# Summing a node's first twelve edges by tile additions in a graph network kernel

## The chip, the cores and the metric

The kernel runs on one core of a Trainium2 chip. The metric is the time of one execution on the device in microseconds, the median of several. PE is TensorE, DVE VectorE, ACT ScalarE, POOL GpSimd, and SP the engine that starts most plain transfers. PEld is PE's loading of weights. L480 means line 480 of the kernel that the profile belongs to, so the same line number means different things before and after.

Each set of runs was given a chip that could not be chosen, and the kernel before met two kinds of them: on one kind it takes about 9670 us, on the other about 8980 us. Within a kind the runs of one kernel agree to about one per cent. I call them the slow and the fast kind. The prediction and the first result are from the slow kind. Numbers are compared only within a kind, except where the text says that it compares the kinds.

## The reference

There are N = 10000 nodes with D = 512 features, and 160000 edges sorted by target, each with one of four types. Layer 0 sends messages of the right type over each edge; layer 1 is two steps of mean aggregation.

```python
h = relu(layernorm(x))
h_all = einsum('nd,rdf->nrf', h, rel_W) + rel_b         # four tables: (10000, 4, 512)
agg = segment_sum(h_all[src, edge_type], dst) / max(deg, 1)
x1 = layernorm(h + h @ self_W + self_b + agg)
x = x + layernorm(x1 + gelu(x1 @ W1 + b1) @ W2 + b2)
h = relu(layernorm(x))
for W_self, W_neigh, b in ((ws1, wn1, bs1), (ws2, wn2, bs2)):
    agg = segment_sum(h[src], dst) / max(deg, 1)
    h = relu(h @ W_self + agg @ W_neigh + b)
out = x + h
```

## The kernel before

The work falls into four stages: products (five 512 x 512 weights for 79 blocks of 128 nodes, into `hall_d`), a pass of sums over `hall_d` with the feed-forward, and a pass each over `h1_d` and `h2_d`. The edge lists are prepared on DVE between the first products and the others. In every pass the sum of a block's edges is the same function: up to 18 gathers of 128 rows, each split in a high and a low part for two fp32r matmuls by a one-hot matrix.

```python
def block_sums(b, table, idx):
    n = caps[b]                                   # 18
    hot = hotp.tile([P, CAP, P], F32R, name="hot")
    nc.vector.tensor_tensor(hot[:, :n], lane..., loc[:, at[b]:at[b] + n]..., op=OP.is_equal)
    pa = psA.tile([P, D], F32, name="pa")
    for t in range(n):
        rows = rowp.tile([P, D], F32, name="rows")          # 12 buffers
        nc.gpsimd.indirect_dma_start(out=rows, in_=table, ...idx[:, w:w + 1]...)
        nc.scalar.copy(hi, rows)
        nc.vector.tensor_tensor(lo, rows, hi.bitcast(F32), op=OP.subtract)
        nc.tensor.matmul(pa, hot[:, t, :], hi, start=(t == 0), stop=False)
        nc.tensor.matmul(pa, hot[:, t, :], lo, start=False, stop=(t == n - 1))
    return pa

# products, of one block (cut)
    for j, w in enumerate([wself] + wrel):
        pm = psM.tile([P, D], F32, name="pm")               # 4 buffers in PSUM
        for k in range(KC):
            nc.tensor.matmul(pm[:r], hT[:, k, :r], w[:, k, :], ...)
        nc.vector.tensor_tensor(ha[:r, j - 1, :], pm[:r], brel[...], op=OP.add)
# feed-forward: for a group of four blocks in one piece, after their four sums (cut)
```

The read-out of `pm` by DVE is what matters later: PE has four such buffers, and if DVE does not read them, PE stands.

## Time and profile before

| what | before |
|---|---|
| median of three runs, profiled span | 9659.56 us, 9616.8 us |
| products end | 2010 us |
| first gather of `hall_d` to first of `h1_d` | 3213 us |
| from there to the end | 4389 us |
| PE, DVE, ACT, POOL busy | 74%, 52%, 34%, 51% |

The table says which stage takes how long, and the shares say that no engine is full over the whole. The prediction shows the same stages engine by engine, and reads from them which engine limits which stage.

### The profile page before, as it was taken

The page shows a single profiled execution, that of the slowest core. Times are in us where ns is not written, and L with a number is a line of the kernel's source. Part 1 is how long each engine was busy: PE and PEld are TensorE (multiplying, and loading weights), DVE is VectorE, ACT ScalarE, POOL GpSimd, SP SyncE. Part 2 cuts the span into 40 slices and gives each one's busy share as a digit, 9 for nine tenths or more (in the row PEclk, how much of TensorE's full clock was granted, in tenths as well). Part 3 has the DMA queues.
Part 4 walks back from the last instruction along what each step waited for, and adds up shares of the span by engine and source line. Part 5 has one row for each costly group of instructions (what it writes and reads, how often), then busy time and mean ns, then how long its engine had stood idle before and what let it go on. Part 6 is the DMA issues. An engine that isn't in the chain of part 4 may idle for free. (4 is left out here: it accounts for less than half of the span.)

```text
span 9616.8 us, 69806 instructions
## 1 busy us (share of the span) xinstructions
PE 7076.1 (74%) x18796; PEld 3705.1 (39%) x18796; DVE 4980.6 (52%) x6861; ACT 3224.2 (34%) x5464; POOL 4946.0 (51%) x4465
## 2 busy tenths in 40 slices
PE   6208999977777777686777767767766777777677
PEld 2103444433333333343334444444443444444344
DVE  6994222244545454545454555555554555555555
ACT  0000000023334343333343444444443444444444
POOL 1001111144546464646463767767665767777666
PEclk8558999978787878787877878888888888888888
DMA  3002222254545454545353666666665666666666
GB/s 110 23 0 92 96 101 109 84 169 135 147 129 154 137 159 132 152 122 165 113 167 111 198 181 194 188 185 194 187 177 179 201 198 201 201 204 204 192 198 181
DMA packets 498906, 1459.78 MB, mean 152 GB/s; under 512 B 90419, under 2 KB 90419, under 8 KB 488371
## 3 DMA queue, kind: packets, MB, share of 16 engines
q0 software_dynamic: 337680, 1106.78, 39.4%
q1 hardware_dynamic: 109330, 191.42, 6.2%
q10 hardware_dynamic: 51488, 157.01, 4.1%
q8 instruction: 150, 2.46, 0.1%
q14 instruction: 258, 2.11, 0.1%
HBM read 1249.45 MB, written 205.45 MB: 151 GB/s over the span
## 5 line engine op out<-in xcount | busy, mean ns | idle before, releaser
L313 POOL DMA_INDIRECT rows<-h_d,idx x2814 | 3038.9, 1080 | 1383.8 <-issue 756.4
L319 DVE TENSOR_TENSOR lo<-rows,hi 128x512 fp32r<-128x512 f32 x4221 | 2803.5, 704 | 1798.0 <-issue 449.5
L318 ACT CAST hi<-rows 128x512 fp32r<-128x512 f32 x4221 | 2467.0, 618 | 3592.9 <-PE pa L320 1612.6
L321 PE MATMUL pa<-lo,hot 128*128 128x512 f32 x4221 | 2321.8, 551 | 537.1 <-DVE lo L319 335.6
L313 POOL DMA_INDIRECT rows<-hall_d,idx x1407 | 1600.7, 1138 | 1444.3 <-DVE lo L319 873.9
L320 PE MATMUL pa<-hi,hot 128*128 128x512 f32 x4221 | 2016.5, 478 | 439.1 <-issue 232.8
L321 PEld LDWEIGHTS pa<-lo,hot 128*128 128x128 f32 x4221 | 909.2, 215 | 1367.0 <-DVE lo L319 647.1
L320 PEld LDWEIGHTS pa<-hi,hot 128*128 128x128 f32 x4221 | 920.9, 218 | 945.1 <-issue 654.5
L187 PE MATMUL pm<-wrel,hT 128*128 128x512 f32 (+1 forms) x2528 | 1115.8, 599 | 42.2 <-DVE xs L193 25.7
L422 PE MATMUL po<-wns,mTb 128*128 128x512 f32 (+1 forms) x1264 | 788.3, 781 | 205.0 <-ACT mTb L150 126.9
L187 PEld LDWEIGHTS pm<-wrel,hT 128*128 128x128 f32 (+1 forms) x2528 | 481.7, 191 | 661.3 <-issue 605.1
L419 PE MATMUL po<-wss,hTb 128*128 128x512 f32 (+1 forms) x1264 | 690.1, 630 | 0.7 <-ACT hTb L150 0.7
L181 POOL TENSOR_TENSOR hg<-hg,bself 128x512 f32<-128x512 f32 (+1 forms) x79 | 99.5, 1280 | 1129.5 <-PE pT L149 1129.5
L149 PE MATMUL pT<-ident,mb 128*128 128x128 f32 (+1 forms) x632 | 142.7, 366 | 708.8 <-ACT mb L414 491.5
L190 DVE TENSOR_TENSOR ha<-pm,brel 128x512 f32<-128x512 f32 (+1 forms) x316 | 218.2, 691 | 764.6 <-PE pm L187 764.6
L306 DVE TENSOR_TENSOR hot<-lane,loc 128x2304 fp32r<-128x2304 f32 (+1 forms) x237 | 602.8, 2544 | 5.6 <-PE pa L320 5.4
L368 PE MATMUL ph<-x1T,w1s 128*128 128x512 f32 (+2 forms) x1344 | 570.6, 586 | 27.0 <-ACT x1T L150 19.1
L422 PEld LDWEIGHTS po<-wns,mTb 128*128 128x128 f32 (+1 forms) x1264 | 308.6, 256 | 636.5 <-issue 448.1
L375 PE MATMUL po<-w2s,hid 128*128 128x512 f32 (+1 forms) x1264 | 548.1, 594 | 0.0
L377 DVE TENSOR_TENSOR xsg<-po,xsg 128x512 f32<-128x512 f32 (+1 forms) x79 | 54.6, 691 | 903.9 <-PE po L375 903.9
L425 DVE TENSOR_TENSOR ob<-po,bss 128x512 f32<-128x512 f32 (+1 forms) x158 | 109.3, 692 | 728.4 <-PE po L422 653.3
L182 POOL TENSOR_TENSOR xg<-xg,ln2b 128x512 f32<-128x512 f32 (+1 forms) x79 | 98.9, 1282 | 648.0 <-ACT hg L178 648.0
(96 smaller groups left out, 4032.9 us busy)
## 6 DMA issues: line engine op xcount, KB each, us to landing
hall_d<-ha ACTq DMA_DIRECT2D x78, 1024.0 KB
rows<-h_d,idx POOLq DMA_INDIRECT x2814
hb<-h_d SPq DMA_DIRECT2D x156, 256.0 KB
rows<-hall_d,idx POOLq DMA_INDIRECT x1407
h_d<-ob ACTq DMA_DIRECT2D x78, 256.0 KB
res<-xn_d SPq DMA_DIRECT2D x78, 256.0 KB
out_dram<-ob ACTq DMA_DIRECT2D x78, 256.0 KB
xg<-in_x_dram SPq DMA_DIRECT2D x19, 1024.0 KB
```

What stands on the lines that cost most here:

```text
L187: nc.tensor.matmul(pm[:r], hT[:, k, :r], w[:, k, :], start=(k == 0), stop=(k == KC - 1))
L190: nc.vector.tensor_tensor(ha[:r, j - 1, :], pm[:r], brel[:r, (j - 1) * D:j * D], op=OP.add)
L306: nc.vector.tensor_tensor(hot[:, :n], lane[:, None, :].to_broadcast([P, n, P]), loc[:, at[b]:at[b] + n].unsqueeze(2).to_broadcast([P, n, P ...
L313: nc.gpsimd.indirect_dma_start(out=rows, out_offset=None, in_=table, in_offset=bass.IndirectOffsetOnAxis(ap=idx[:, w:w + 1], axis=0))
L318: nc.scalar.copy(hi, rows)
L319: nc.vector.tensor_tensor(lo, rows, hi.bitcast(F32), op=OP.subtract)
L320: nc.tensor.matmul(pa, hot[:, t, :], hi, start=(t == 0), stop=False)
L321: nc.tensor.matmul(pa, hot[:, t, :], lo, start=False, stop=(t == n - 1))
L368: nc.tensor.matmul(ph[:, :n], w1s[:, k, f * P:(f + 1) * P], x1T[:, k, :n], start=(k == 0), stop=(k == KC - 1))
L375: nc.tensor.matmul(po[:r], hid[:, f, c * r:(c + 1) * r], w2s[:, f, :], start=(f == 0), stop=(f == FC - 1))
L419: nc.tensor.matmul(po[:r], hT[:, k, :r], wss[:, k, :], start=(k == 0), stop=False)
L422: nc.tensor.matmul(po[:r], mT[:, k, :r], wns[:, k, :], start=False, stop=(k == KC - 1))
```

## The change

Its intent is to leave most of the one-hot work out. A node's first 12 edges are gathered so that edge j of node p lands on partition p of tile j; tiles are then summed with plain additions. Only the further edges of a block (room for 720, six tiles) go through the one-hot, with plain fp32 matmuls. To find each node's first edge, the ends of the runs of equal targets are found by twelve top-eight passes, scattered to memory, read back and spread by a running maximum. That work is issued step by step between the products. The feed-forward is cut into quarters that go between the sums.

```diff
+    T = 3 * E // (4 * N)                    # 12
+    OV = 720
+    def edges(ep, ep2, pse):                # a generator: one step after each block of products
 ...
+        for j in range(n8):                 # 96 scatters of run ends
+            st = nc.gpsimd.indirect_dma_start(out=end_d, ...to_i[:, j:j + 1]..., in_=end_f[:, j:j + 1])
+        yield
+        nc.sync.dma_start(eb, end_d[:NE, :]...)
+        nc.vector.tensor_tensor_scan(run, eb, eb, 0.0, op0=OP.max, op1=OP.max)
 ...
+        for b in range(NB):                 # 79 gathers of 12 records a node
+            nc.gpsimd.indirect_dma_start(out=row0[:, b, :], in_=rec_d, ...first_i[:, b:b + 1]...)
 ...
+                for t in range(len(ov_tiles(b))):      # 469 gathers of one record a partition
+                    nc.gpsimd.indirect_dma_start(out=ovr0[:, b, t:t + 1], in_=rec_d, ...)
+            if b0 == 0:
+                nc.vector.copy_predicated(row0, few, nowhere...)
+        yield
+        nc.vector.tensor_scalar(ovr1[:, :NB - 1, :], ovr0[:, :NB - 1, :], 2, None,
+                                op0=OP.logical_shift_right)
 ...
         def products(g):
 ...
-                nc.gpsimd.tensor_tensor(h, h, bself[:r], op=OP.add)
+                nc.vector.tensor_tensor(h, h, bself[:r], op=OP.add)
+                next(step, None)
 ...
+        def fold(b, halves, left):
+            nc.vector.tensor_tensor(t[:r], t[:r], u[:r], op=OP.add)           # 3072 columns
+            while n > left:
+                nc.vector.tensor_tensor(t[:r, :m, :], t[:r, :m, :], t[:r, n - m:n, :], op=OP.add)
 ...
+        for i, (o, n) in enumerate(others):
+            nc.tensor.matmul(pa[:r], hot[:n, i, :r], o[:n], start=(i == 0), stop=(i == last))
 ...
+            for bs in plan:                 # a quarter of the feed-forward after each block's sum
+                    if queue:
+                        fed = queue.pop(0)()
```

## The prediction

> **What bounds the kernel now.** I read the page's slices, then a table of busy time by stage, then the groups, then stretches of the timeline. The stages follow from the first and last instruction of a line: products with the five weights (line 187) end at 2010 us, gathers from hall_d run from 2014.8 to 5143, those from h1_d from 5227.9, those from h2_d from 7441 to 9591. Cut there (columns: stretch, its length, busy us of PE, PEld, DVE, ACT, POOL, granted clock, DMA share, GB/s):
> ```profile
> 0.00:274.00 274.00, 187.25 (x420) 81.23 (x421) 172.07 (x344) 19.39 (x31) 35.48 (x33) 0.89 0.33 116
> 274.00:766.00 492.00, 47.30 (x169) 40.02 (x167) 492.00 (x157) 0.59 (x1) 3.77 (x3) 0.51 0.00 0
> 766.00:2012.00 1246.00, 1235.12 (x3050) 554.82 (x3050) 291.94 (x516) 90.75 (x148) 159.92 (x129) 1.00 0.25 99
> 2012.00:5228.00 3216.00, 2410.19 (x5746) 1204.58 (x5747) 1642.90 (x2562) 1215.08 (x1997) 1707.91 (x1487) 0.79 0.47 143
> 5228.00:7441.00 2213.00, 1604.65 (x4703) 926.48 (x4701) 1184.97 (x1644) 946.58 (x1643) 1521.67 (x1407) 0.82 0.64 186
> 7441.00:9616.00 2175.00, 1591.53 (x4710) 897.93 (x4710) 1196.66 (x1642) 951.84 (x1644) 1517.20 (x1407) 0.84 0.67 199
> ```
> Four limits show. Row two: DVE is busy all 492 us, with the products waiting behind it. Row three: PE is full at clock 1.00. Row four: nobody is full. The last two: POOL is at 69 and 70%. But POOL is closer to its limit than that share says, because the issue gap between gathers isn't counted as busy. Two stretches of POOL's timeline (start, duration, instruction, idle before it and its cause):
> ```profile
> 5238.01 0.95 POOL L313 DMA_INDIRECT rows<-h_d,idx  x1 [0.30 <-issue]
> 5239.26 0.95 POOL L313 DMA_INDIRECT rows<-h_d,idx  x1 [0.30 <-DMA rows<-h_d,idx]
> ...
> 2160.72 0.95 POOL L313 DMA_INDIRECT rows<-hall_d,idx  x1 [0.30 <-issue]
> 2211.55 0.95 POOL L313 DMA_INDIRECT rows<-hall_d,idx  x1 [49.89 <-DVE lo L319]
> ```
> An undisturbed gather costs POOL 0.95 + 0.30 = 1.25 us whatever it moves. Eighteen make 22.5 us a block of 128 nodes, 1755 us for 78 blocks. In the second stretch POOL stands 49.89 us: the twelve row buffers are full while PE works through the feed-forward of four blocks in one piece. That is the first pass's excess over the other two.
>
> The groups give the rest (busy, mean ns, idle before):
> ```profile
> L313 POOL DMA_INDIRECT rows<-h_d,idx x2814 | 3038.9, 1080 | 1383.8 <-issue 756.4
> L319 DVE TENSOR_TENSOR lo<-rows,hi 128x512 fp32r<-128x512 f32 x4221 | 2803.5, 704 | 1798.0 <-issue 449.5
> L313 POOL DMA_INDIRECT rows<-hall_d,idx x1407 | 1600.7, 1138 | 1444.3 <-DVE lo L319 873.9
> L306 DVE TENSOR_TENSOR hot<-lane,loc 128x2304 fp32r<-128x2304 f32 (+1 forms) x237 | 602.8, 2544 | 5.6 <-PE pa L320 5.4
> ```
> The mean gather is 1080 or 1138 ns, not 946 (the median). The timeline shows why; of both engines, in one stretch:
> ```profile
> 2288.43 2.52 DVE L306 TENSOR_TENSOR hot<-lane,loc 128x2304 fp32r<-128x2304 f32 x1
> 2288.61 3.17 POOL L313 DMA_INDIRECT rows<-hall_d,idx  x1 [0.30 <-DVE mvb L138]
> ```
> A gather that started just after a DVE operation with two SBUF inputs ended some 0.8 us after that operation, 2.2 us late.
>
> **What the Trainium skill says.** "SBUF — State Buffer", section "Who interferes with whom": a DVE instruction with two SBUF inputs contends with a GpSimd instruction that reads SBUF, and the later one blocks. The trace agrees: the stretch of (1.080 - 0.946) x 2814 + (1.138 - 0.946) x 1407 = 647 us. "TensorE: Matmul & The Clock Gate", section "What's actually happening": idle throttles PE, activity releases it. Agrees: 0.51 beside an idle PE, 1.00 beside a full one. So the clock of 0.8 in the passes is a sign of PE's slack and not a fixed price. "FP8 and Floating Point Precision" says that true fp32 takes four passes through the array. In the trace a fp32 512-column matmul is two instructions (2528 records for 1264 matmuls), which start 0.43 us apart at full clock, so 0.86 us; a fp32r one starts 0.23 us after another, which agrees roughly (3.7 times).
>
> **The change, part by part.**
>
> Gathers: still 12 + 6 = 18 a block (the last block 13 instead of 3), the same 1.25 us each. That floor doesn't move, and it decides.
>
> Edges and products. Removed from DVE: 78 comparisons of 1250 columns (1.45 us) and 78 pairs of one-hot and reduction (2.55 + 4.0 us), 624 us in all. Added: 12 top-eight passes with replacement, an estimate of 12 x 3 = 36 us from 1250 columns at 1.45 us a sweep, and 79 comparisons of 768 columns, under 1 us each. Two adds a block (2 x 0.69) come from POOL. All of it is issued between blocks of products; DVE had only 292 us of work in 1246 us of products, so PE keeps its 17.9 us a block (40 x 0.43 plus transposes): 27 + 79 x 17.9 = 1441 us. PE also gets 474 narrow matmuls, some 50 us. POOL gets 96 scatters and 79 + 469 small gathers, 644 x 1.25 = 805 us, from about 200 us on: hidden, unless DVE waits for the scatters in order (up to 100 us). Products end at about 1510 us instead of 2010: 500 us saved.
>
> Passes over h1 and h2. DVE loses 18 x 0.70 us of remainders and 2.55 us of one-hot a block, ACT 18 x 0.62 us of casts; neither was the bound. PE: 36 fp32r at 0.23 = 8.4 us become (6 + 3) x 0.86 = 7.7 us: no change. DVE gets the fold: 3072 columns, then 1536, at the one-hot's rate (2304 columns in 2.55 us) 3.3 and 1.7 us, both with two SBUF inputs. A gather comes to its read every 1.25 us, on average 0.6 us after the first add began; so it is held 3.3 - 0.6 = 2.7 us, and the next by 0.3 us in the second add. The smaller one-hot costs 0.3 us. So 22.5 + 3.3 = 25.8 us a block, 78 x 25.8 + 13 x 1.25 = 2030 us, plus 28 us from the last gather to the next pass: 2058 instead of 2213 and 2055 instead of 2175. Saved: only 155 + 120 us.
>
> Pass over hall_d. PE needs per block 12 x 0.43 for the sums, 32 x 0.43 for a quarter of feed-forward and 1.1 for transposes: 20.0 us at full clock, 23.5 at 0.85. POOL needs 22.5 + 3.0 for the fold + 0.9 for the last small adds and the 0.7 us operations of the norms: 26.4 us, and loses b2's add (1.39 us). The quarter between two sums is shorter than the two blocks of gather buffers (45 us), so the 49.9 us stands should go. With 0.6 us for PE nearly level with POOL: 27 us x 78 + 16 = 2122 us, plus a drain of five quarters, about 85 us as against 85 today (5143 to 5228). So 2207 instead of 3216: 1010 us saved.
>
> Sum: 1510 + 5 + 2207 + 2058 + 2055 = 7835 us; I say 7830.
>
> **Rivals.**
> 1. No lock loss: the fold is one long operation a block instead of 18 short ones, and gathers slip between. Then 22.5 us a block and 3 x 1770, about 7000 us. Against it: the 2.52 us one-hot above held its gather to the end.
> 2. The lock holds across the whole chain of adds, not to the end of each: the fold costs 4.4 us in the last two passes and 6 in the first, 27.2 and 29.5 us a block: about 8250 us. For it: gathers of up to 11.25 us in the first pass, and 2293.45 held 7.58 us by adds back to back. Against it: counted over the trace, 206 of the 228 gathers over 1.5 us ended 0.82 us after the end of the first such operation that they met. I weigh it at one in five.
> 3. PE becomes the bound in the first pass: at clock 0.8 it needs 25 us and waits for the last gather of a block before the quarter starts. Pass one goes to 29 or 30 us a block, in all about 8050 us. For it: the old clock of 0.79. Against: the clock rises when PE has no long idle.
> 4. The transfers: 18 gathers move 4.6 MB in 26 us, with loads some 215 GB/s; the third pass already moves 199 at a DMA share of 0.67. Not the bound.
> 5. The edge work doesn't hide: DVE stands at the read-back of the run ends, products end at 1650, in all 7970 us.
>
> **Range and chances.** Rival 2, 3 and 5 lie above, 1 below; half of rival 1 and all of 2 in the range: 7350 to 8250 us. For a change within 2% nearly all the first pass's and the edges' 1500 us must come back, which nothing here suggests; only a failed fit (the data miss the 720 slots and the general branch runs) would. Faster 0.98.
>
> **What would show it.** Right: no stretch of DVE alone before the products, PE full until about 1500; POOL's idle before gathers near 0.30 us each in all passes, no wait near 50 us; the gathers' mean 1.10 to 1.15 us, with one of about 3.5 us a block beside the fold. Wrong: gathers' mean under 1.0 (rival 1) or over 1.25 us (rival 2); POOL waiting for the fold or PE in the first pass (rival 3); PE idle at 200 to 500 us (rival 5).

## The result, and the profile after

| | before | after | predicted for after |
|---|---|---|---|
| median | 9678.06 us | 8584.87 us | 7830 us |
| products end | 2010 us | 2210 us | 1510 us |
| pass over `hall_d` | 3213 us | 2181 us | 2207 us |
| the last two passes | 4389 us | 4157 us | 4113 us |

The changed kernel is right in its outputs and faster: ratio 0.8873, interval 0.8821 to 0.8925. A ratio is the mean time of one kernel's runs over that of the other's of the same rounds, so not quite the ratio of the medians quoted. But the time lies far above the range that I gave. The table tells where: the three passes came out within 2% of their predicted lengths, and the products came out 700 us too long, longer even than before. This is the table of busy time by stage of the changed kernel (columns as in the prediction), cut where POOL starts and stops issuing the small transfers of the edge work:
```profile
147.00:224.00 77.00, 0.27 (x2) 0.06 (x1) 3.31 (x5) 0.58 (x1) 58.40 (x62) 0.53 0.10 28
224.00:340.00 116.00, 112.25 (x269) 50.28 (x269) 34.04 (x71) 6.46 (x11) 5.56 (x6) 0.95 0.21 82
340.00:440.00 100.00, 41.15 (x119) 17.21 (x118) 13.30 (x27) 2.00 (x4) 75.37 (x79) 0.68 0.11 26
440.00:556.00 116.00, 110.17 (x459) 51.89 (x458) 56.96 (x105) 8.88 (x15) 0.00 (x0) 0.94 0.28 109
556.00:865.00 309.00, 66.94 (x180) 26.21 (x179) 14.55 (x23) 1.17 (x2) 233.84 (x240) 0.57 0.04 7
865.00:975.00 110.00, 92.73 (x351) 42.06 (x351) 44.31 (x80) 9.50 (x15) 0.43 (x1) 0.85 0.27 104
975.00:1269.00 294.00, 89.30 (x172) 37.33 (x170) 18.21 (x32) 4.40 (x7) 223.15 (x229) 0.64 0.07 20
1269.00:2214.00 945.00, 906.22 (x2236) 405.63 (x2236) 272.45 (x469) 67.50 (x110) 0.05 (x2) 0.98 0.24 95
2214.00:4395.00 2181.00, 1698.10 (x3862) 748.70 (x3862) 1242.84 (x1672) 458.10 (x652) 1627.44 (x1417) 0.90 0.66 206
4395.00:8552.00 4157.00, 2899.51 (x6616) 1243.39 (x6616) 1144.32 (x789) 289.55 (x474) 3232.71 (x2834) 0.84 0.66 200
```
The reader is to compare the first number after each length (PE) with the fifth (POOL). Where POOL issues, PE does 0.27 of 77, 41 of 100, 67 of 309 and 89 of 294 us. In the rows between, where POOL has nothing to do, PE is busy 84 to 97% of the time. The last two columns say that it is not the memory: the transfers move next to nothing there. The granted clock falls to 0.53 to 0.68 in the same rows, as it did beside an idle PE in the prediction's table (0.51). It is too little to be the cause: a step of 0.43 us would take 0.81 us at 0.53 of the clock (an estimate from these numbers), and the steps shown next are 2.80 us apart.

So the products, which were to hide the edge work, stood while it went on. The question is why. Two stretches of that time, DVE's and PE's (start, duration, instruction, and in brackets the idle time before it and what ended it):
```profile
167.25 0.69 DVE L420 TENSOR_TENSOR ha<-pm,brel 128x512 f32<-128x512 f32 x1 [19.71 <-remote]
189.65 0.69 DVE L420 TENSOR_TENSOR ha<-pm,brel 128x512 f32<-128x512 f32 x1 [21.71 <-remote]
```
```profile
645.89 1.01 PE L417 MATMUL pm<-wrel,hT 128*128 128x512 f32 x1 [1.79 <-issue]
648.69 1.01 PE L417 MATMUL pm<-wrel,hT 128*128 128x512 f32 x1 [1.79 <-issue]
```
DVE reads out a product every 22.40 us, which is eight matmuls (four fp32 ones, two instructions each) 2.80 us apart; at full speed they are 0.43 us apart. And in this stretch PE waits for nothing that the profile shows ("issue"). This looked like an engine that gets its instructions slowly, and it led me first to theory S: **TensorE steps slowly as long as GpSimd issues small transfers**. Its rival, theory W, is the fifth rival of the prediction: **an instruction in DVE's order waits for a small transfer, and the read-out of the products stands behind it.**

The passes first, since there the prediction's steps can be seen to hold. The gathers and the first addition on the page (busy us, mean ns of one, idle before):
```profile
L453 POOL DMA_INDIRECT half<-h_d,row x1896 | 1902.3, 1003 | 719.4 <-issue 568.6
L453 POOL DMA_INDIRECT half<-hall_d,row x948 | 1072.5, 1131 | 1250.2 <-DMA ovr<-rec_d,at_i 945.6
L461 POOL DMA_INDIRECT other<-h_d,ovr x938 | 1330.4, 1418 | 285.8 <-issue 280.9
...
L480 DVE TENSOR_TENSOR half<-half 128x3072 f32<-128x3072 f32 (+1 forms) x237 | 795.7, 3358 | 703.3 <-DMA half<-h_d,row 308.8
```
And one block's additions with the gathers beside them, in the timeline:
```profile
6006.99 0.94 POOL L461 DMA_INDIRECT other<-h_d,ovr  x1 [0.30 <-issue]
6007.79 3.36 DVE L480 TENSOR_TENSOR half<-half 128x3072 f32<-128x3072 f32 x1 [4.43 <-DMA half<-h_d,row]
6008.24 3.73 POOL L461 DMA_INDIRECT other<-h_d,ovr  x1 [0.30 <-issue]
6011.19 1.76 DVE L483 TENSOR_TENSOR half<-half 128x1536 f32<-128x1536 f32 x1
6012.28 1.49 POOL L461 DMA_INDIRECT other<-h_d,ovr  x1 [0.30 <-issue]
```
An undisturbed gather still costs 0.94 + 0.30 us, and one that starts 0.45 us into the first addition takes 3.73 us, to 0.82 us after the addition's end. The next one is held to the end of the second addition in the same way, each by its own operation. The time that the gathers of the last two passes take above 945 ns each sums to (1.003 - 0.945) x 1896 + (1.418 - 0.945) x 938 = 554 us, 3.5 us for each of 158 blocks; I had predicted 3.3.

### The profile page after: what moved, and what is told of

Its sections match the earlier page's. It is cut to its first block, busy times and chain, and to the rows that moved or that the text cites.

```text
span 8551.8 us, 44099 instructions
## 1 busy us (share of the span) xinstructions
PE 6091.4 (71%) x14444; PEld 2657.9 (31%) x14444; DVE 2916.0 (34%) x3393; ACT 858.3 (10%) x1306; POOL 5490.2 (64%) x4911
## 5 line engine op out<-in xcount | busy, mean ns | idle before, releaser
L493 PE MATMUL pa<-other,hot 128*128 128x512 f32 (+2 forms) x2814 | 1808.9, 793 | 1587.8 <-DMA other<-h_d,ovr 848.8
L453 POOL DMA_INDIRECT half<-h_d,row x1896 | 1902.3, 1003 | 719.4 <-issue 568.6
L453 POOL DMA_INDIRECT half<-hall_d,row x948 | 1072.5, 1131 | 1250.2 <-DMA ovr<-rec_d,at_i 945.6
L461 POOL DMA_INDIRECT other<-h_d,ovr x938 | 1330.4, 1418 | 285.8 <-issue 280.9
L493 PEld LDWEIGHTS pa<-other,hot 128*128 128x128 f32 (+2 forms) x2814 | 653.8, 251 | 2598.0 <-issue 1842.4
L480 DVE TENSOR_TENSOR half<-half 128x3072 f32<-128x3072 f32 (+1 forms) x237 | 795.7, 3358 | 703.3 <-DMA half<-h_d,row 308.8
L364 POOL DMA_INDIRECT ovr<-rec_d,at_i x469 | 457.5, 975 | 371.7 <-DVE at_i L361 225.7
L461 POOL DMA_INDIRECT other<-hall_d,ovr x469 | 554.9, 1183 | 143.2 <-issue 113.6
L483 DVE TENSOR_TENSOR half<-half 128x1536 f32<-128x1536 f32 (+2 forms) x395 | 525.9, 1331 | 13.6
L496 PE MATMUL pa<-half,ident 128*128 128x512 f32 (+1 forms) x948 | 438.1, 598 | 2.2 <-DVE half L483 2.2
```

What stands on the lines that cost most here:

```text
L364: nc.gpsimd.indirect_dma_start(out=ovr0[:, b, t:t + 1], out_offset=None, in_=rec_d, in_offset=bass.IndirectOffsetOnAxis(ap=at_i[:, b - b0, ...
L453: nc.gpsimd.indirect_dma_start(out=t[:r, j, :], out_offset=None, in_=table, in_offset=bass.IndirectOffsetOnAxis(ap=row[:r, b, i * H + j:i ...
L461: nc.gpsimd.indirect_dma_start(out=o[:n], out_offset=None, in_=table, in_offset=bass.IndirectOffsetOnAxis(ap=ovr[:n, b, t:t + 1], axis=0))
L480: nc.vector.tensor_tensor(t[:r], t[:r], u[:r], op=OP.add)
L483: nc.vector.tensor_tensor(t[:r, :m, :], t[:r, :m, :], t[:r, n - m:n, :], op=OP.add)
L493: nc.tensor.matmul(pa[:r], hot[:n, i, :r], o[:n], start=(i == 0), stop=(i == last))
```

## The experiments

Eighteen kernels were run, and all were correct.

### 1. Do gathers issued beside the products slow TensorE? (fast kind, kernel before 8968.76)

The kernel before with bself's and ln2b's additions on DVE as after (p0), and with 474 gathers added whose result nobody reads: of 4-byte rows (p1), of 2048 bytes (p2), of 512 bytes (p3).
```diff
-                nc.gpsimd.tensor_tensor(h, h, bself[:r], op=OP.add)
+                nc.vector.tensor_tensor(h, h, bself[:r], op=OP.add)
+        for j in range(474):                              # p1; p2, p3 with wider rows
+            nc.gpsimd.indirect_dma_start(out=junk[:, j:j + 1], in_=rec_d, ...idx1[:, j:j + 1]...)
```

> Control for the three probes: the kernel before, with the two adds a block of the products stage moved from POOL to DVE, so that POOL does nothing there. All theories: the stage from 766 us to the last product stays about 1246 us, at clock 1.00, and the whole stays near 9620 us; DVE has over 900 us of slack in the stage.

> The control plus 474 gathers of 4-byte rows, 128 rows each, into a column that nothing reads, issued by POOL back to back beside the products; nothing of PE, DVE or ACT waits for them. Theory A (indirect DMAs with tiny rows slow PE itself while POOL issues them): PE makes a quarter of its normal progress for the 590 us that they take, so the products end some 400 us later and the whole is near 10,000 us. Rival B (in the changed kernel PE was held by the order of the edge work on DVE and its waits, the gathers do nothing): no change, within 30 us of the control.

> The control plus 474 gathers of 2048-byte rows from x into tiles that nothing reads, in the same place. Theory A with the row size as the cause: no slowing, as in the passes, where PE runs 34 matmuls in a row beside such gathers: within 50 us of the control. If any indirect DMA beside full PE load slows PE: some 400 us more, as with 4-byte rows.

> The control plus 474 gathers of 512-byte rows. If there is a step between 4 and 2048 bytes, this says on which side 512 lies: either about 400 us later than the control or within 50 us of it. I expect it nearer to the 2048-byte case.

Measured: 8999.11, 8969.12, 9001.38 and 8975.91 us; the products end at 2003, 2002, 2011 and 2005 us. Nothing slowed by more than 8 us. Two flaws keep these runs from settling it. The gathers ran from 287 us on, and more than half of them beside a PE that was idle anyway. And, as showed only in the next set, this was the fast kind of chip.

### 2. The additions cut, and fewer gathers (slow kind, kernel before 9673.5, three rounds)

The changed kernel again (r0); the fold's additions cut into pieces of 512 columns (a1); room for 640 further edges of a block in place of 720, so 17 gathers a block in place of 18 (a3; the fullest block of these data has 637); both (a5).
```diff
-            nc.vector.tensor_tensor(t[:r], t[:r], u[:r], op=OP.add)                 # a1, a5
+            for i in range(n):
+                nc.vector.tensor_tensor(t[:r, i, :], t[:r, i, :], u[:r, i, :], op=OP.add)
-    OV = 720                                                                        # a3, a5
+    OV = 640
```

> The changed kernel itself again, beside the kernel before, which took 8969 us here and not 9678. Theory A' (the products stage stalls through something of the changed kernel's own, its tiny indirect DMAs beside its order of waits): the products end near 2210 us again, PE doing one instruction in 0.7 to 1.4 us while POOL scatters and gathers. Rival C (the stall belongs to the chip of the first measurement, as does part of its slower passes): the products end near 1500 us as I predicted, and the whole comes to 7800 us.

> The changed kernel with every add of the fold cut into adds of 512 columns: the same work on DVE (some 0.3 us more a block), in operations of 0.6 us instead of 3.3 and 1.7. Theory L (a gather is held to the end of the one DVE operation that it meets): the mean of the gathers from h falls from 1003 (halves) and 1418 ns (others) to under 1050 both, the block from 26.3 to about 24 us, the last two passes together from 4157 to about 3800 us. Rival M (the hold lasts over a chain of adds back to back): no gain, the one held gather a block still takes 4 to 5 us.

> The changed kernel with room for 640 instead of 720 further edges a block (the data's fullest block has 637): five gathers of further edges instead of six, 17 a block instead of 18. If POOL's 1.25 us a gather bounds the passes: 78 x 3 x (1.25 + a little hold) = about 300 us less in all, 100 us a pass. If PE bounded the first pass: nothing there, about 200 us in all. The products stage gets 78 gathers less, at most 90 us.

> Both edits. If both count on POOL they add: about 300 + 400 us less than the changed kernel in the passes. The first pass stops at PE's 20 us a block at full clock, near 23 us at the granted one, so it may gain less.

| | median us | ratio to before | products end | pass over `hall_d` | last two passes |
|---|---|---|---|---|---|
| r0_same | 8590.12 | 0.8881 | 2209 | 2215 | 4159 |
| a1_split | 8857.35 | 0.9161 | 2209 | 2481 | 4113 |
| a3_ov640 | 8187.96 | 0.8469 | 2099 | 2138 | 3930 |
| a5_both | 8311.28 | 0.8589 | 2098 | 2312 | 3905 |

The first result repeats: products to 2209 again. One gather fewer a block is worth 402 us here. In the profiled runs it is 110 in the products (78 small gathers fewer), 77 in the first pass and 229 in the other two. In these two POOL's 1.25 us an issue make 156 x 1.25 = 195 of it. Cutting the additions did what it should to the hold: the mean of a further gather of `h_d` fell from 1438 to 939 ns. And yet the kernel became 267 us slower. Its trace shows POOL and PE in one stretch of the last pass but one:
```profile
6007.75 0.95 POOL L453 DMA_INDIRECT half<-h_d,row  x1 [0.30 <-issue]
6014.67 0.94 POOL L453 DMA_INDIRECT half<-h_d,row  x1 [5.98 <-PE pT L160]
```
```profile
6010.00 0.27 PE L160 MATMUL pT<-ident,hb 128*128 128x128 f32 x1 [1.68 <-issue]
6012.10 0.37 PE L160 MATMUL pT<-ident,hb 128*128 128x128 f32 x1 [1.83 <-issue]
6013.50 0.37 PE L160 MATMUL pT<-ident,hb 128*128 128x128 f32 x1 [1.03 <-issue]
6014.20 0.37 PE L160 MATMUL pT<-ident,hb 128*128 128x128 f32 x1 [0.33 <-issue]
```
PE's four small transposes start 2.10, 1.40 and 0.70 us apart, multiples of 0.70, although nothing that the profile shows holds them; the next four, of mb, start 0.67 us after these and take 1.12 us together. POOL then waits for PE. So theory S's slow steps turn up in the passes as well. Summed over the three passes, the idle time of PE that `prof <label> --waits` puts down to issue grows from 584 us in r0 to 905 in a1 (from 498 in a3 to 754 in a5), while the time that the gathers of the last two passes take above 945 ns each falls from 562 to 81 us. That fits a loss by slow steps. Whether it is one, or the price of more and shorter additions, set 5 tells.

### 3. The changed kernel on the fast kind (kernel before 8985.03)

The changed kernel (r1); p1's gathers again, but made to depend on the degrees, so that all run from 799 to 1398 us beside products at full clock (p4); the changed kernel with an addition of 256 columns on POOL after each of the 644 small transfers (a6); the changed kernel with all the edge work issued before the products (a2).
```diff
+        nc.vector.tensor_scalar(idxj, idx1[:, :474], late, None, op0=OP.add)     # p4; late from rdeg
+            nc.gpsimd.tensor_tensor(pad, zero[:, :256], col..., op=OP.add)        # a6, 644 times
-        next(step)                                                                # a2: moved down
-        for g in groups:
-            products(g)
         for _ in step:
             pass
+        for g in groups:
+            products(g)
```

> The changed kernel once more, to see which kind of chip this call got: the first call's chip ran the kernel before in 8969 us, the second call's in 9674. Where the kernel before takes 9650: 8590 us and products that end at 2210. Where it takes 8970: if PE's slow steps are the chip's, products near 1500 us and a whole of 7800; if they are the kernel's, 2210 again.

> The first probe put right: its 474 gathers of 4-byte rows ran half beside an idle PE. Now their indices wait for the degrees, so that all run beside the products at full clock. Theory S (on such a chip PE falls to steps of 0.7 us while POOL issues indirect DMAs without a pause, whatever the rows are): on a 9650-us chip the products end about 400 us later than 2010, on an 8970-us chip not at all. Rival B (the order of the edge work in the changed kernel): within 30 us of 2010 on either.

> The changed kernel with a small add on POOL (256 columns, it reads what the DMA's indices came from) after each of the 644 scatters and gathers of the edge work. Theory S, if a pause of POOL is what frees PE: the slow steps go or thin out, the products end several hundred us before 2210, though POOL's own work grows by 644 x 0.8 = 500 us. If a pause of this size isn't enough: POOL's longer work keeps PE slow for longer, products near 2500 us.

> The changed kernel with the edge work issued before the products instead of between them. If the two hinder each other only through PE's slow steps, products still overlap where the engines' order lets them, and the end stays within 100 us of 2210, or earlier if PE is left idle while POOL issues and then runs 79 x 17.9 us undisturbed: 1270 + 1415 = 2690 us at the latest.

Measured: r1 8313.88 us, p4 8992.1, a6 8565.42, a2 8315.73; the products end at 1957, 2003, 2196 and 1983 us. p4 answers what p1 left open: on this kind of chip 474 gathers beside full products cost the products nothing (2003 as without them). So theory S does not hold on the fast kind. And the products of r1 still end at 1957, 447 us after the predicted 1510. Issuing the edge work first (a2) doesn't help; its trace has three long idle times of PE too, 75, 55 and 335 us. Slowing POOL (a6) makes it worse: the four long idle times of PE in a6's trace, 106 + 82 + 244 + 242 = 674 us, are 233 us more than the three of r1, 63 + 48 + 331 = 442 by rounded parts, and the products end 239 us later. But the 244 are of my making: DVE's L364 waits 255 us for the paced additions on POOL, which read the tile that it writes. The other three come to 430 us, no more than r1's. So a6 shows that PE stands when an instruction in DVE's order waits for POOL, and doesn't show that slower small transfers cost more. The trace of the changed kernel on the fast kind then shows the waits themselves. It is shown here from r2 of the next set, which has them within 2 us of r1's. DVE's timeline:
```profile
757.67 0.69 DVE L420 TENSOR_TENSOR ha<-pm,brel 128x512 f32<-128x512 f32 x1 [2.74 <-PE pm L417]
1100.66 0.40 DVE L376 TENSOR_SCALAR ovr<-ovr 128x468 int32<-128x468 int32 x1 [342.30 <-DMA ovr<-rec_d,at_i]
1101.68 0.15 DVE L378 TENSOR_SCALAR ovr<-ovr 128x1 int32<-128x1 int32 x1 [0.61 <-DMA ovr<-rec_d,at_i]
1101.75 1.28 DVE L420 TENSOR_TENSOR ha<-pm,brel 128x512 f32<-128x512 f32 x2
```
and PE's:
```profile
767.77 3.60 PE L417 MATMUL pm<-wrel,hT 128*128 128x512 f32 x8
1102.48 3.92 PE L417 MATMUL pm<-wrel,hT 128*128 128x512 f32 x5 [331.12 <-DVE ha L420]
```
At 758 us DVE comes to the shift of the further edges' rows (L376). It needs the last of the 469 small gathers, and POOL, at 1.25 us each, is through with them at 1100. The shift's result isn't needed before the second pass. But DVE works in order; the read-outs behind it stand for 342 us, PE fills its four PSUM buffers and stands for 331. Two more waits of the kind are in the same trace: 75 us for the read-back of the run ends (PE stands 63) and 58 us at the masking of the rows (PE 50).

The Trainium skill says just this of the order: "PSUM — Partial Sum Buffer", section "Engine vs sequencer instructions", calls the queues of ScalarE, VectorE and GpSimd strict FIFO. The trace agrees, with the 342 us above: DVE passed over nothing that stood behind L376 and was ready. The timelines also show that the instructions don't stand where the source has them. The masking is emitted after the first 40 blocks' counts, and in DVE's timeline it comes before the end of these (422 us in r2, with counts of the first 40 blocks behind it). So instructions are moved ahead of their place in the source; by which rule, no run here shows.

On the slow kind the same three instructions don't wait at all. In the trace of the first result DVE comes to them late, behind the slow products, at 246, 460 and 1346 us; the last scatter, the last gather of a node's records and the last further gather start at 230, 439 and 1268 us. DVE's timeline has no idle time before the shift:
```profile
1344.98 0.69 DVE L420 TENSOR_TENSOR ha<-pm,brel 128x512 f32<-128x512 f32 x1 [2.74 <-PE pm L417]
1345.59 0.39 DVE L376 TENSOR_SCALAR ovr<-ovr 128x468 int32<-128x468 int32 x1
```
So theory W describes the fast kind alone. In the first result the waits cost nothing (r0 shows the same), and what is seen there is theory S's slow steps.

### 4. The waits taken away (fast kind, kernel before 8994.28, three rounds)

To place an instruction late its operands have to say so; a version that only wrote the three later in the source had them in the same places in the compiled order, one block later at most, and was not run. So a one-column copy from a late product goes into the tile that the instruction overwrites. b0 does it with the shifts alone, b1 with all three waits, b2 is b1 with room for 640.
```diff
+                newest[0] = xs[:, c, 0:1]                     # after each block of products
+        while len(newest) < 2:                                # until the last product
+            yield
+        nc.vector.tensor_copy(ovr1[:N % P, 0, 0:1], newest[1][:N % P])          # b0, b1, b2
+        nc.vector.tensor_copy(ovr1[:N % P, NB - 1, 0:1], newest[1][:N % P])
         nc.vector.tensor_scalar(ovr1[:, :NB - 1, :], ovr0[:, :NB - 1, :], 2, None, ...)
+        nc.vector.tensor_copy(few[:N % P, 0, 0:1], newest[1][:N % P])           # b1, b2: masking
+        nc.vector.tensor_copy(run[:, 0:1], newest[0][:NB])                      # b1, b2: read-back
```

> The changed kernel once more, as the yardstick of the three others of this call, and to see which kind of chip this is. Two kinds were met: on one the kernel before takes about 9670 us and the changed kernel's products end at 2209; on the other 8980 and 1957. Here I expect one of these two pairs, and a ratio of 0.888 or 0.926.

> VectorE's shift of the further edges' rows, at which it stood 342 us for the last of 469 small gathers on the fast chip (with the products standing 331 us behind it), is tied to the last block of the products and so comes after them; nothing else is changed. Theory W (VectorE meets instructions that wait for small transfers in its order, and the products' read-out stands behind them): on the fast kind of chip the products end at 1957 - 331 = 1626 and the whole is 330 us shorter than the changed kernel in the same call, about 0.96 of it. Theory S (TensorE steps slowly as long as GpSimd issues small transfers, whoever waits): products end where the changed kernel's do; on the slow kind of chip, where TensorE was already slow in that stretch, I expect 2209 less at most 50.

> All three waits of that kind taken away: the read-back of the run ends comes after block 16, the masking of the rows and both shifts after the last product. W: on the fast kind the products end at 1957 - 331 - 48 - 63 = 1515, the passes keep 2180 and 4170, total 7870 or 0.947 of the changed kernel. S: the gathers of 814 us still run beside the products; on the slow kind TensorE did 224 us of work in 825 us of such stretches, so the products end above 2050 there although nobody waits; W alone would say about 1520 there too.

> The same with room for 640 further edges of a block instead of 720, so that GpSimd issues 17 gathers for a block and not 18. Expected better than both kernels: on the slow kind this room took the time after the products from 6378 us to 6072, about 300 less, so on the fast kind 7870 less about 290 = 7580, ratio to before 0.845; on the slow kind under S about 8100, ratio 0.84.

| | median us | ratio to before | products end | pass over `hall_d` | last two passes |
|---|---|---|---|---|---|
| r2_same | 8292.33 | 0.9221 | 1955 | 2175 | 4164 |
| b0_ovr_late | 7953.41 | 0.8849 | 1622 | 2175 | 4151 |
| b1_all_late | 7855.6 | 0.8739 | 1525 | 2180 | 4145 |
| b2_late_640 | 7553.75 | 0.8407 | 1522 | 2100 | 3913 |

The waits were worth what the trace said: 333 us of the products for the shifts (331 expected) and 97 more for the other two (111 expected). The passes did not change. b1's table by stage, in the rows where POOL issues and after them:
```profile
109.00:232.00 123.00, 121.88 (x307) 55.13 (x305) 34.36 (x57) 10.84 (x17) 93.76 (x96) 1.00 0.24 86
...
521.00:1113.00 592.00, 587.30 (x1660) 267.63 (x1659) 201.10 (x352) 46.68 (x76) 448.77 (x469) 1.00 0.29 105
1113.00:1525.00 412.00, 408.45 (x1014) 180.67 (x1012) 120.72 (x205) 28.53 (x47) 0.00 (x0) 1.00 0.23 91
1525.00:3709.00 2184.00, 1709.72 (x3862) 740.22 (x3862) 1246.45 (x1674) 457.03 (x652) 1654.10 (x1417) 0.90 0.67 206
3709.00:7854.00 4145.00, 2902.79 (x6616) 1245.29 (x6616) 1144.28 (x789) 277.07 (x474) 3236.56 (x2834) 0.85 0.67 200
```
PE is busy 587 of 592 us beside POOL's 469 gathers, at full clock. This is the picture that the prediction described, and the products end at 1525 where it said 1510. Theory W holds on the fast kind; without the waits the products are within 15 us of the prediction.

### 5. The last two (fast kind, kernel before 8988.75, three rounds)

c0 is b1 again, for the case that it met the slow kind; c1 is b2 with a1's cut of the additions.

> The kernel with all three waits taken away, once more. On the fast kind of chip again 7856 us, products to 1525, ratio 0.874. On the slow kind: theory S (TensorE steps slowly while GpSimd issues transfers, whoever waits) has the products end above 2050 and the whole at about 8450; theory W alone has them end at about 1525 and the whole at about 7900.

> The best version so far (waits taken away, room for 640) with the additions of the first twelve edges cut into pieces of 512 columns, so that no gather is held for 3 us. On the slow kind of chip this cut removed the hold and made the passes 220 us longer, because TensorE fell into slow steps. If those steps belong to that kind of chip, then on the fast kind the hold's time comes back: it is 138 + 385 us in the second and third pass and 273 in the first, so up to 800 us, of which the extra VectorE instructions take some; I expect 7100 us, ratio 0.79. If undisturbed issue slows TensorE on every chip, no gain: 7550 or more.

c0: 7865.08 us, ratio 0.8752; it was the fast kind again, so it only repeats b1. c1: **7074.33 us, ratio 0.7873** (0.7859 to 0.7886), the fastest of all and better than both kernels. Its products end at 1523, its first pass takes 2085 us (b2 2100), its last two 3461 (b2 3913). So nearly all of the gain is in the last two passes. In the first, POOL then waits 162 us for additions to free the buffers of its gathers (33 us in b2). The groups of gathers of `h_d` in the trace of c1 up to 7000 us:
```profile
L462 POOL DMA_INDIRECT half<-h_d,row x1872 | 1771.4, 946 | 721.0 <-issue 530.4 <-DMA h_d<-h 126.3 <-DMA h_d<-ob 25.0
L470 POOL DMA_INDIRECT other<-h_d,ovr x771 | 787.6, 1022 | 235.0 <-issue 204.2 <-DMA half<-h_d,row 30.5 <-PE pT L160 0.3
```
The means are 946 and 1022 ns, in b2 over its whole trace 1016 and 1437: the hold is nearly gone. Over the whole of both traces, the time that the gathers of the last two passes take above 945 ns each falls from 519 to 62 us, by 457, and the two passes become 452 us shorter. The same cut on top of room for 640 made the kernel 123 us slower on the slow kind (a3 to a5) and makes it 479 us faster here, with the waits taken away as well (ratios 0.8407 to 0.7873, of two sets). So the loss in a1 and a5 was no price of the cut itself, such as the time of more and shorter additions. It belongs to the slow kind of chip, as the slow steps in a1's trace do: in the passes of c1 no idle time of PE is put down to issue.

## Why the prediction was wrong

- **The step that failed** is the one on edges and products: PE "keeps its 17.9 us a block", and POOL's 644 scatters and gathers are "hidden, unless DVE waits for the scatters in order (up to 100 us)". In the result PE did not keep its pace. In the four stretches of the table in which POOL issues, PE worked 198 of 780 us, with one matmul instruction every 2.80 us in place of 0.43 where a stretch is shown, and the products ended at 2210 in place of 1510. The waits of DVE, which the step had made its exception, were not what happened there: the three instructions came late and did not wait. Why PE steps slowly there is open. (The terms that the working names sum to 27 + 1414 + 50 = 1491 us; the other 19 of the 1510 are not explained.)
- **On the fast kind** the same step fails by the exception itself, and that is shown by experiments. Three such waits turn up and not one, and the long one isn't the one that I looked at. They cost PE 63 + 50 + 331 us, and taking them away brought the products from 1955 to 1525. I had named the mechanism as the fifth rival, at 140 us for the products, and had sized only the read-back of the scatters. The working already had the number for the others: 469 gathers at 1.25 us are 586 us, and I didn't ask which DVE instruction needs the last of them and where it stands in DVE's order.
- **What tells the kinds apart** in the traces is idle time of PE that is put down to issue. In the passes of the kernel before it is 696 us on the slow kind and 21 in p0, on the fast; of the changed kernel, 465 us in the products and 571 in the passes on the slow kind, 0 and 26 in r2. So the sign stood in the trace that the prediction read, and was not asked about. On the slow kind it comes with POOL's issuing, in steps at multiples of 0.70 us; p4, r2, b1 and c1 show the same issuing on the fast kind without it. What makes the kinds differ is open. Neither p4 nor a kernel without the waits met a slow chip; since nothing waited there, taking the waits away should gain nothing there, but this was not run.
- **The pass over `hall_d`** was right: 2181 us (fast kind 2175) against 2207. PE's clock in it rose from 0.79 to 0.90 as argued, and the 29 or 30 us a block of rival 3 (2300 us and more) are out.
- **The last two passes** were right: 4157 us (fast kind 4164) against 4113. But what they save depends on the kind. The kernel before takes 4389 us for them on the slow kind and 3989 on the fast (p0, whose passes are those of the kernel before), so on the fast kind the change made them 175 us longer, and its gain there is in the pass over `hall_d` (3000 to 2175). POOL's issue sets the pace: a gather fewer a block took 229 us off them on the slow kind (r0 to a3) and 232 on the fast one (b1 to b2).
- **The hold by additions** was right in kind and size: 3.5 us a block against 3.3, to the end of one addition and not of the chain. That rules out rival 2, and rival 1's free passage as well. That it binds is shown by c1: cutting the additions took these passes from 3913 to 3461 us on the fast kind.
- **The range** was drawn to the second rival's 8250, and the fifth stood in it with 140 us. Had that rival been sized as above, at 444 us, it would have stood at 8274, a little past the range and still 311 us short of the result. The terms of the sum of 7830 are all found in b1 (products to 1525, 2180, 4145; in all 7856 with the few us between), on the fast kind and with the waits taken away.

## What to carry to other kernels

Before calling a stream of small transfers hidden, list the instructions that wait for its last member, and find each one's place in the order of its engine: whatever that engine does for the bottleneck afterwards stands as long. If such an instruction is not needed yet, tie it to something late, since the scheduler may move it ahead of where it was written. Ask of a trace what an engine's idle time put down to nothing is, before taking its pace from it. And repeat a result on more than one chip before explaining it: a cut that costs 123 us on one kind of chip gained 479 on the other (there with the waits taken away).

## What the Trainium skill lacked or had wrong

- "SBUF — State Buffer", section "Who interferes with whom", infers that a two-input tensor_tensor does not hold the descriptor generation of a GpSimd transfer, because it takes only the read interface of the shared ports. The runs show an indirect gather held: 3.73 us in place of 0.94 beside a 3.36 us addition, and a mean of 1438 ns that fell to 939 (slow kind) when the additions were cut. They don't tell whether the generation is what is held or the reading of the gather's indices, so they leave the inference open for a plain transfer. The rule of the same section, that the order of issue decides who blocks, agrees: the gather began second and was held.
- No page that I found gives the pace at which POOL issues indirect transfers back to back: 0.945 + 0.30 = 1.25 us each, the same for 4 bytes and for 2048 a row. "DMA: Bandwidth & Descriptors", section "Anatomy of one DMA — SWDGE (gpsimd) path", calls the generation small and puts most of a fixed time of about 2.0 us in the completion; here the issue sets the pace of the last two passes (a gather fewer a block took 232 us off them on the fast kind).
- No page that I found has the slow steps of PE: starts at multiples of 0.70 us while POOL issues transfers, on chips where one kernel takes 9670 us in place of 8980.
